# Sums of four softmax weights in all groups but the last batch's, and query and key stacks through a DRAM copy, in a planned graph-network kernel

## The chip, the cores and the metric

One core of one Trainium2 chip runs the whole program. Time is device microseconds of one execution. The engines named below: PE is the tensor engine (PEld are its weight loads), DVE the vector engine, ACT the scalar engine, POOL the GpSimd engine, SP the engine that issues most of the DMAs. SBUF and PSUM are the on-chip memories, DRAM the memory outside the core.

## What is computed

Sixteen graphs (batches) of 1024 nodes with 256 features, all with one 1024 x 1024 adjacency matrix, go through four layers, each on `relu(layernorm(x))` with a residual. Layers 0 to 2 are graph attention layers (4 heads, 1 head, 1 head). Layer 3 is the one that the change touches; cut to what matters:

```
x -> h = max(layernorm(x), 0)
q, k, v = split(h @ w_qkv), 8 heads of 32
scores  = q k^T / sqrt(32), where(adj > 0, scores, -1e9)
t       = softmax(scores) @ v
y       = layernorm(h + t);  f = relu(y @ w1 + b1) @ w2 + b2
x + layernorm(y + f)
```

All is in float32.

## The kernel before

`direct` builds the kernel. It doesn't issue instructions in the order of the source: it records pieces of work, each with its engine, an assumed duration, the buffers that it reads and writes, and a place in a stream. `Record.schedule` then goes through a model of the engines and writes the order in which all of them are issued, for every engine. Engines work through their own list in order. The constants `PASS`, `SLACK`, `BIAS`, `LEAD` and the lists in `KNOTS` (one per stream, interpolated along the stream) set priorities and assumed delays; the streams of one batch's graph layers (`gat0` to `gat2`) and of another batch's layer 3 (`values`, `steps`, `feed`) run beside each other. The last batch has no other beside it.

Layer 3 (`attention`) works in four groups per batch: two sets `g` of four heads, and two halves `hf` of the 512 queries each. A group has eight steps `jt`, one for each 128 keys. A step makes the scores of four heads (L1352, on PE), their exponentials (L1376, on ACT) into two tiles `pa` of 128 x 2 x 512, and the product with the 0/1 mask (L1385, on DVE). Two steps later the weights are used twice on PE, each time by a "quad": four narrow matmuls of 32 columns each that lie side by side (L1217, eight instructions, as a float32 matmul is two).

- One quad multiplies them with the values, for each step.
- Another multiplies them with `ones`, which gives the softmax's denominators. It need not see each step alone: `run_of` says how many steps' weights are added up first, in a pair of tiles `sums`. The first two are added on DVE (L1244), and each further one by an accumulating DMA that POOL issues (L1253), two DMAs per step, one for each tile of the pair. There is one pair of `sums`, with two tiles, which the next run takes over after the quad.

Before, a run has 4 steps in the groups with `hf` = 1 and 2 steps in those with `hf` = 0; in the last batch there is no adding.

The scores' operands are stacks: queries and keys are split into a rounded part `hi` and a rest `lo` and laid over each other on the partitions, four blocks `a` of 32 rows (queries hi, hi, lo, lo; keys hi, lo, hi, lo), for each of the four heads `r`. `project` makes one half of them: a matmul (L1132), `hi` on ACT (L1141), `lo` on DVE (L1144), and then 16 DMAs on SP's queue, one for each block and head, from SBUF to SBUF (L1154). There are 8 projections per batch. `hi` and `lo` have one buffer each, the keys' stack `ks` one and the queries' stack `qs` two.

Other work on the queues: SP also issues the stores of graph attention's rows to DRAM (L843, `rd<-rt`), their broadcast back to all partitions (L852, `row<-rd`, which L868 on DVE waits for), loads of `x`, and the feed-forward part's loads and stores (L1502, L1574). POOL also computes the layer norms' powers (L466, L481) and some sums of the range watch (L511, L820).

Of the kernel before, what the change touches and what calls it, by code (L numbers as in the profile page):

```python
# [113 lines left out]


WEIGHT = {"pe": 1.0, "dve": 0.3}
PASS = {"pe": 0.198, "act": 0.153, "dve": 0.202, "pool": 0.13, "dma": 0.0}


class Work:  # L120


    def __init__(self, engine, us, emit, key, modes, moved, lands):
        self.engine, self.us, self.emit, self.key, self.modes = engine, us, emit, key, modes
        self.pass_on = PASS[engine]
        self.moved = moved
# [9 lines left out]
def priority(x):  # L136
    base, knots, total, lead = x.stream
    at = x.pos / max(total, 1e-9) * (len(knots) - 1)
    k = max(0, min(int(at), len(knots) - 2))
    key = base + knots[k] + (knots[k + 1] - knots[k]) * (at - k)  # L140
    return round(key - (LEAD.get(x.engine, 0.0) if lead else 0.0), 6)


class Record:
# [44 lines left out]
    def schedule(self):  # L189
        for n, x in enumerate(self.work):  # L190
            x.n = n
            if x.key is None:
                x.key = priority(x)
            x.left = len(x.before)
            for y in x.before:
                y.after.append(x)
        free = dict.fromkeys(PASS, 0.0)
        queue = 0.0
        future = {e: [] for e in PASS}
        now = {e: [] for e in PASS}  # L200
        mode = "full"
        for x in self.work:
            if not x.left:
                heapq.heappush(future[x.engine], (x.ready, x.n, x))

        def opening(x):

            at, need = 0.0, {}
            for buf in x.opens:
                need[buf.ring] = need.get(buf.ring, 0) + 1  # L210
            for ring, n in need.items():
                if len(ring.free) < n:
                    return None
                at = max(at, sorted(ring.free)[n - 1][0])
            return at

        def turn(x):

            return BIAS * SWITCH.get((mode, x.modes[0]), 0.0) if x.engine == "pe" else 0.0

        def choose(e):

            at = free[e]
            while future[e] and future[e][0][0] <= at:
                x = heapq.heappop(future[e])[2]
                heapq.heappush(now[e], (x.key, x.n, x))
            best = None
            for key, n, x in now[e]:
                t = opening(x)
                if t is not None:  # L230
                    best = min(best or (1e9,), (max(at, t), key + turn(x), n, x))
            if future[e] and (best is None or future[e][0][0] < best[0]):
                for t, n, x in sorted(future[e]):
                    if opening(x) is not None:
                        t = max(t, at, opening(x))
                        best = min(best or (1e9,), (t, x.key + turn(x), n, x))
                        break
            return best

        order = []  # L240
        while True:
            choices = [(c, e) for c, e in ((choose(e), e) for e in PASS) if c]
            if not choices:
                break
            (at, _, n, x), e = min(choices, key=lambda c: c[0][0])
            if (x.key, n, x) in now[e]:
                now[e].remove((x.key, n, x))
                heapq.heapify(now[e])
            else:
                future[e].remove((x.ready, n, x))  # L250
                heapq.heapify(future[e])
            for buf in x.opens:
                _, k = heapq.heappop(buf.ring.free)
                buf.k, buf.t = k, buf.ring.tiles[k]
            us = x.us
            if e == "pe":
                us += SWITCH.get((mode, x.modes[0]), 0.0)
                mode = x.modes[1]
            x.start = at
            if x.moved:  # L260
                queue = max(at + (us if e == "pool" else 0.2), queue) + x.moved
                us = max(us, queue - at - AHEAD)
                x.pass_on = queue + x.lands + SLACK - (at + us)
            order.append(x)
            free[e] = at + us
            for buf in x.shared:
                buf.end = max(buf.end, at + us + x.pass_on)
                buf.uses.remove(x)
                if not buf.uses:
                    heapq.heappush(buf.ring.free, (buf.end, buf.k))  # L270
            for y in x.after:
                y.ready = max(y.ready, at + us + (x.pass_on if y.before[x] else 0.0))
                y.left -= 1
                if not y.left:
                    heapq.heappush(future[y.engine], (y.ready, y.n, y))
        assert len(order) == len(self.work)
        self.end = max(free.values())
        return order


AHEAD = 3.5
SLACK = 0.56
KNOTS = {
    "gat0": (-6.706, -3.534, -2.307, -1.522, -2.815),
    "gat1": (0.005, 0.503, 0.618, 0.731, 0.916),
    "gat2": (0.938, 0.468, 0.637, 0.867, 1.15),
    "beside": (0.241, 1.203, 1.943, 0.54, 4.121),
    "values": (1.06, -3.362, -0.305, 3.145, 0.767),
    "steps": (1.014, 1.448, 1.59, 2.064, 1.794),
    "feed": (2.016, 2.165, 2.509, 2.154, 2.609),  # L290
    "last": (2.808, 3.335, 3.547, 5.206, 6.138),
}
BIAS = 1.225
LEAD = {"act": 9.55, "dve": -0.732}

SWITCH = {
    ("full", "col4"): 0.137,
# [23 lines left out]
def mm_us(n):  # L321
    return 2 * max(2 * n / 2.4 + 3.0, 109) / 1000
# [5 lines left out]
def direct(ctx, tc, flag, x, adj, gat_w, gat_a, w_qkv, ln1_g, ln1_b, ln2_g, ln2_b, w1, b1, w2, b2, out):  # L328


    nc = tc.nc
    NB, N, C = x.shape
    NT = N // P
    CT = C // P
    HALF = N // 2
    TH = NT // 2
    D3 = C // H3
    HG = P // D3
# [31 lines left out]
    def ring(name, n, shape, pool=work):  # L370
        return Ring([pool.tile([P] + shape, F32, name=f"{name}{i}") for i in range(n)])
# [32 lines left out]
    dram = ctx.enter_context(tc.tile_pool(name="dram", bufs=1, space=DRAM))  # L404
    r_x3 = ring("x3", 3, [NT, C], dram)
    r_rd = ring("rd", 4, [P], dram)
    r_rt = ring("rt", 1, [P])
    r_sc = ring("sc", 4, [HALF], psum)
    r_bank = Shared([psum.tile([P, HALF], F32, name=f"bank{i}") for i in range(4)])
# [8 lines left out]
    def pe(us, emit, w, r, modes=("full", "full")):  # L418
        rec.add("pe", us, emit, w, r, modes)

    def act(us, emit, w, r):
        rec.add("act", us, emit, w, r)
# [7 lines left out]
    def dma(moved, lands, emit, w, r, key=None, us=0.57, engine="dma"):  # L430
        rec.add(engine, us, emit, w, r, key=key, moved=moved, lands=lands)
# [650 lines left out]
    def attention(b, xt, b_mv, b_rstd):  # L1082
# [42 lines left out]
        def project(g, hf, keys, stack, at):  # L1125

            sc, hi, lo = r_sc.new(), r_hi.new(), r_lo.new()
            c0 = keys * C + g * P

            def product():  # L1130
                for ct in range(CT):
                    nc.tensor.matmul(  # L1132
                        sc.t,
                        wqkv_sb[:, ct, c0 : c0 + P],
                        hT.t[:, ct, hf * HALF : (hf + 1) * HALF],
                        start=ct == 0,
                        stop=ct == CT - 1,
                    )

            pe(CT * mm_us(HALF), product, [sc], [b_qkv] + [hT((ct, hf)) for ct in range(CT)])  # L1140
            act(act_us(HALF), lambda: nc.scalar.copy(hi.t.bitcast(F32R), sc.t), [hi], [sc])  # L1141
            dve(
                tt_us(HALF),
                lambda: nc.vector.tensor_sub(lo.t, sc.t, hi.t),  # L1144
                [lo],
                [sc, hi],
            )
            for a in range(4):
                part = ((hi, hi, lo, lo), (hi, lo, hi, lo))[keys][a]
                for r in range(HG):  # L1150
                    dma(
                        0.3,
                        1.5,
                        lambda: nc.sync.dma_start(  # L1154
                            stack.t[a * D3 : (a + 1) * D3, r, at : at + HALF],
                            part.t[r * D3 : (r + 1) * D3, :],
                        ),
                        [stack((r, hf if keys else 0, a))],
                        [part],
                        us=0.59,  # L1160
                    )

        def values(it):
            sc = r_sc.new()
# [47 lines left out]
        steps = [(g, hf, jt) for g in range(CT) for hf in range(2) for jt in range(NT)]  # L1212
# [11 lines left out]

        def run_of(g, hf):

            return 1 if b == NB - 1 else 4 if hf == 1 else 2

        rec.stream(b, KNOTS["steps"])
        GROUP = 2  # L1230
# [1 line left out]
        for n in range(len(steps) + LAG):  # L1232
            m = n - LAG
            if m >= 0:
                g, hf, jt = steps[m]
# [12 lines left out]
                elif jt % run:  # L1248
                    for ss, pt in zip(sums[g, hf], pas[m]):
# [6 lines left out]
                            us=1.135,  # L1256
# [81 lines left out]
            if n < len(steps):  # L1338
                g, hf, jt = steps[n]
# [928 lines left out]
```

## Time and profile before

| What | Value |
|---|---|
| Median of 3 runs | 4092.49 us (4090.72 to 4097.2) |
| The profiled execution | 4091.28 us, its span 4089.5 us |
| Mean granted clock of PE | 0.995 |
| PE: sum quads of `sums` with `ones` | 1440 instructions, 193.4 us busy |
| DVE: adds into `sums` | 360, 430.3 us |
| POOL: accumulating DMAs | 240, 512 KB each |
| SP: copies for the stacks | 2048, 64 KB each |

How to read it: busy time of an engine is the time in which an instruction of it ran; a matmul's end is modelled and matmuls overlap, so the time that a matmul costs PE is read from start to start. In lines of the groups the parts are line, engine, operation, out<-in, shapes, count, then busy time in us and mean ns of one, then the idle time of the engine ahead of them and what ended it. In lines of the waits: who waited, for whom, the total in us, how often, the longest. In lines of a timeline: start in us, duration, engine, line, operation, out<-in, shape, count.

### The profile page before, as it was taken

Reading aid. Unit: us, or ns where it says so; the run is one execution under the profiler, and the core shown is the slowest. Engines: PE = TensorE matmul, PEld = TensorE weight load, DVE = VectorE, ACT = ScalarE, POOL = GpSimd, SP = SyncE. Lnnn points to the kernel's source line nnn. Section 1 sums busy time; section 2 is a strip of 40 time slices with the busy share of each in tenths; the row PEclk is TensorE's granted clock in tenths of the full one; section 3 lists DMA queues with packets and bytes.
Section 4 is the critical chain, followed back from the end, with each engine's and each line's share of the span. In section 5 each row is a group of like instructions: output and inputs, shape, how many; then the busy total and the mean of one; then the engine's idle time right before and its main releaser. Section 6 shows DMA issues by size and latency. Waiting matters only on the chain.

```text
span 4089.5 us, 68377 instructions
## 1 busy us (share of the span) xinstructions
PE 4023.3 (98%) x23874; PEld 2354.7 (58%) x23874; DVE 3499.0 (86%) x5994; ACT 2689.9 (66%) x6673; POOL 646.7 (16%) x631
## 2 busy tenths in 40 slices
PE   7999999999999999999999999999999999999998
PEld 3566466564655646566564665646556465665643
DVE  7768898988979799897988989889797998979866
ACT  5467676775757767576675767757577675765765
POOL 1102011121211202111121211212111011111100
PEclk9999999999999999999999999999999999999999
DMA  3024344343444324443243443434443244432441
GB/s 128 24 77 102 99 109 99 89 93 98 101 112 102 90 75 112 114 108 90 77 105 99 109 105 87 95 92 103 110 109 85 74 112 113 108 90 59 107 103 47
DMA packets 215248, 389.65 MB, mean 95 GB/s; under 512 B 45168, under 2 KB 80240, under 8 KB 214896
## 3 DMA queue, kind: packets, MB, share of 16 engines
q1 hardware_dynamic: 180336, 259.36, 22.4%
q0 software_dynamic: 34560, 125.84, 16.2%
q8 instruction: 191, 3.13, 0.3%
q14 instruction: 161, 1.32, 0.1%
HBM read 91.03 MB, written 33.95 MB: 31 GB/s over the span
## 4 chain that ended last, share of the span: by engine, by line
PE 85%; DVE 5%; ACT 4%; SPq 2%; DMA 2%; issue 1%; POOL 1%; DVEq 0%; ACTq 0%; POOLq 0%
PE bank L895 20%; PE bank L1217 14%; PE sc L1352 11%; PE bank L982 9%; PE bank L770 9%; PE bank L529 6%; PE bank L992 5%; PE bank L1449 4%; PE sc L1132 4%; PE sc L1169 2%; SPq L1154 2%; DVE pt L868 2%; DVE pa L1385 1%; POOL rstdz L466 1%; ACT waste L446 1%
## 5 line engine op out<-in xcount | busy, mean ns | idle before, releaser
L1385 DVE TENSOR_TENSOR pa<-pa,mask 128x1024 f32<-128x1024 f32 x1024 | 1221.4, 1218 | 72.4 <-ACT pa L1376 69.4
L1376 ACT ACTIVATE pa<-sc 128x512 f32<-128x512 f32 x2048 | 1098.3, 606 | 234.2 <-PE sc L1352 175.1
L868 DVE SCALAR_TENSOR_TENSOR pt<-row,e,mask 128x512 f32<-128x512 f32 x1472 | 1016.3, 744 | 62.2 <-DMA row<-rd 40.3
L895 PE MATMUL bank<-qb,pt 128*128 128x257 f32 x4096 | 942.0, 380 | 3.5 <-ACT fz L1533 3.5
L895 PEld LDWEIGHTS bank<-qb,pt 128*128 128x128 f32 x4096 | 771.3, 189 | 147.1 <-ACT pa L1376 12.6
L1352 PE MATMUL sc<-qs,ks 128*128 128x512 f32 x2048 | 717.7, 455 | 11.2 <-DMA qs<-lo 5.8
L1217 PE MATMUL bank<-pa,va 128*32 128x512 f32 x4096 | 504.8, 596 | 0.3 <-DVE pa L1385 0.2
L1352 PEld LDWEIGHTS sc<-qs,ks 128*128 128x128 f32 x2048 | 360.4, 189 | 212.3 <-ACT pa L1376 56.5
L1244 DVE TENSOR_TENSOR sums<-pa,pa 128x1024 f32<-128x1024 f32 x360 | 430.3, 1219 | 57.6 <-PE bank L1217 57.4
L982 PE MATMUL bank<-pt,qb 128*32 128x512 f32 x3840 | 468.7, 597 | 2.4 <-DVE pt L868 1.4
L770 PE MATMUL bank<-w_aug,hT 128*128 128x259 f32 (+1 forms) x1504 | 383.1, 393 | 0.5 <-ACT hT L764 0.5
L1253 POOL DMA_DIRECT2D sums<-pa x240 | 210.1, 878 | 930.5 <-DVE pa L1385 507.2
L770 PEld LDWEIGHTS bank<-w_aug,hT 128*128 128x128 f32 x1504 | 275.8, 191 | 121.1 <-ACT pa L1376 13.7
L923 ACT ACTIVATE ex<-bank,rec 128x256 f32<-128x256 f32 x256 | 122.1, 477 | 294.5 <-DVE rec L915 287.6
L982 PEld LDWEIGHTS bank<-pt,qb 128*32 128x32 f32 x3840 | 118.8, 109 | 275.9 <-issue 193.0
L1217 PEld LDWEIGHTS bank<-pa,va 128*32 128x32 f32 x4096 | 120.5, 109 | 263.0 <-issue 227.6
L992 PE MATMUL bank<-pt,e 128*32 128x512 f32 x1920 | 258.5, 592 | 0.0
L500 ACT ACTIVATE hn<-xh,mv,rstd 128x256 f32<-128x256 f32 x376 | 195.9, 592 | 93.0 <-DVE mv L490 89.1
L1132 PE MATMUL sc<-hTa,wqkv_sb 128*128 128x512 f32 x512 | 244.4, 600 | 0.1
L466 POOL TENSOR_TENSOR rstd<-rstd,neg_half 128x4 f32<-128x4 f32 x96 | 138.5, 1443 | 597.0 <-DVE rstd L458 588.3
L820 POOL TENSOR_TENSOR sum_e<-sum_e,e 128x12 f32<-128x12 f32 (+1 forms) x94 | 114.7, 1220 | 648.2 <-ACT e L781 648.1
L1141 ACT CAST hi<-sc 128x512 fp32r<-128x512 f32 x128 | 74.8, 585 | 196.4 <-PE sc L1132 72.8
(152 smaller groups left out, 4638.4 us busy)
## 6 DMA issues: line engine op xcount, KB each, us to landing
sums<-pa POOLq DMA_DIRECT2D x240, 512.0 KB, 6.0
row<-rd SPq DMA_DIRECT2D x184, 256.0 KB
ks<-hi SPq DMA_DIRECT2D x512, 64.0 KB
ks<-lo SPq DMA_DIRECT2D x512, 64.0 KB
qs<-hi SPq DMA_DIRECT2D x512, 64.0 KB
qs<-lo SPq DMA_DIRECT2D x512, 64.0 KB
xh<-in_x_dram SPq DMA_DIRECT2D x32, 512.0 KB
x<-xh SPq DMA_DIRECT2D x32, 512.0 KB
```

The lines of the kernel that those rows point to most:

```text
L529: nc.tensor.transpose(dst(k), src(k), ident[:shape, :shape])
L770: nc.tensor.matmul(g.t[:, : C + 3 * H], hT.t[:, ct, k * P : (k + 1) * P], w_aug[l][:, ct, :], start=ct == 0, stop=ct == CT - 1,)
L868: lambda: nc.vector.scalar_tensor_tensor(pt.t, row.t, e3[:, 2, jt // TH, h, jt % TH : jt % TH + 1], mask[:, jt, hf * HALF : (hf + 1) * HAL ...
L895: nc.tensor.matmul(g.t[:, : D + 1], pts[jt].t[:, k * P : (k + 1) * P], qb[:, jt, 0, :], start=jt == 0, stop=jt == NT - 1,)
L982: nc.tensor.matmul(g.t[u * D + d : u * D + d + D3, :], qb[:, j, h + u, d : d + D3], pts[u][j - jt].t, start=j == 0, stop=j == NT - 1,)
L992: nc.tensor.matmul(gd.t[c : c + D3, :], one(jt + k, h + u).to_broadcast([P, D3]), pts[u][k].t, start=jt == 0, stop=jt == NT - 2,)
L1132: nc.tensor.matmul(sc.t, wqkv_sb[:, ct, c0 : c0 + P], hT.t[:, ct, hf * HALF : (hf + 1) * HALF], start=ct == 0, stop=ct == CT - 1,)
L1217: nc.tensor.matmul(ac.t[r * D3 : (r + 1) * D3, :], columns(r), of_head(r), start=first, stop=last,)
L1244: lambda: nc.vector.tensor_add(ss.t, p0.t, p1.t),
L1352: nc.tensor.matmul(scs[r - r0].t, ks.t[:, r, jt * P : (jt + 1) * P].bitcast(F32R), q.t[:, r, :].bitcast(F32R), start=True, stop=True,)
L1376: lambda: nc.scalar.activation(pt.t[:, v, :], sc.t, AF.Exp, scale=1.0 / math.sqrt(D3)),
L1385: lambda: nc.vector.tensor_mul(pt.t, pt.t, mask[:, jt : jt + 1, i0 : i0 + HALF].to_broadcast([P, 2, HALF]),),
```

## The change

Runs are 4 steps in all groups of all batches but the last, which still adds nothing. `project` stores `hi` and `lo` to a DRAM buffer `hl` (two DMAs) and loads each of the four blocks `a` for all four heads at once from there (four DMAs); SP still issues them all. The planner's constants are others, most of its lists of knots have nine entries in place of five, and its rule for DMAs differs: where a DMA of SP would find the modelled queue more than `BEHIND` us behind, it is assumed to hold SP for `HELD` us, in place of the earlier rule with `AHEAD`.

```diff
-PASS = {"pe": 0.198, "act": 0.153, "dve": 0.202, "pool": 0.13, "dma": 0.0}
+PASS = {"pe": 0.168, "act": 0.548, "dve": 0.19, "pool": 0.13, "dma": 0.0}
...
             if x.moved:
+                if e == "dma" and queue - at > BEHIND:
+                    us = max(us, HELD)
                 queue = max(at + (us if e == "pool" else 0.2), queue) + x.moved
-                us = max(us, queue - at - AHEAD)
                 x.pass_on = queue + x.lands + SLACK - (at + us)
...
-AHEAD = 3.5
-SLACK = 0.56
+BEHIND, HELD = 2.0, 1.35
+SLACK = 0.748
 KNOTS = {
...
-    "steps": (1.014, 1.448, 1.59, 2.064, 1.794),
+    "steps": (0.801, 1.295, 1.336, 1.535, 1.758, 1.892, 2.342, 1.964, 2.258),
...
-BIAS = 1.225
-LEAD = {"act": 9.55, "dve": -0.732}
+BIAS = 1.1
+LEAD = {"act": 10.244, "dve": 1.51}
...
+    r_hl = ring("hl", 3, [2, HALF], dram)
...
+            hl = r_hl.new()
+            for k, part in enumerate((hi, lo)):
+                dma(0.65, 1.5, lambda: nc.sync.dma_start(hl.t[:, k, :], part.t), [hl(k)], [part])
             for a in range(4):
-                part = ((hi, hi, lo, lo), (hi, lo, hi, lo))[keys][a]
-                for r in range(HG):
-                    dma(
-                        0.3,
-                        1.5,
-                        lambda: nc.sync.dma_start(
-                            stack.t[a * D3 : (a + 1) * D3, r, at : at + HALF],
-                            part.t[r * D3 : (r + 1) * D3, :],
-                        ),
-                        [stack((r, hf if keys else 0, a))],
-                        [part],
-                        us=0.59,
-                    )
+                k = ((0, 0, 1, 1), (0, 1, 0, 1))[keys][a]
+                dma(
+                    1.0,
+                    1.83,
+                    lambda: nc.sync.dma_start(
+                        stack.t[a * D3 : (a + 1) * D3, :, at : at + HALF],
+                        hl.t[:, k, :].rearrange("(r d) n -> d r n", r=HG),
+                    ),
+                    [stack((r, hf if keys else 0, a)) for r in range(HG)],
+                    [hl(k)],
+                )
...
         def run_of(g, hf):
 
-            return 1 if b == NB - 1 else 4 if hf == 1 else 2
+            return 1 if b == NB - 1 else 4
```

## The prediction

> **What bounds the kernel now.** I read the page's busy times first, then five equal stretches in the middle, then the tensor engine's (PE's) timeline, then the DMA views, then the waits.
>
> ```profile
> PE 4023.3 (98%) x23874; PEld 2354.7 (58%) x23874; DVE 3499.0 (86%) x5994; ACT 2689.9 (66%) x6673; POOL 646.7 (16%) x631
> ```
>
> Of the span of 4089.5 us PE is without work for 66.2 us. The stretches say where: one batch takes about 248 us, and a stretch of that length from the middle shows
>
> ```profile
> 1618.00:1866.00 248.00, 247.44 (x1483) 146.65 (x1483) 219.31 (x374) 167.92 (x419) 41.13 (x41) 1.00 0.41 99
> ```
>
> PE 247.44 of 248.00 us, at a granted clock of 1.00, VectorE (DVE) 219.31, ScalarE 167.92, the DMA engines 0.41 of the time. So in the middle there is 0.6 us per batch to win from better feeding; the idle 66 us lie mostly in the first 100 us and the last 200. Anything that leaves PE's list of work shortens the batch, as long as nothing else comes to feed it late.
>
> Matmuls overlap, so "busy" might hide gaps. The timeline's starts settle that:
>
> ```profile
> 1507.27 1.04 PE L770 MATMUL bank<-w_aug,hT 128*128 128x259 f32 x4
> 1507.95 0.82 PE L1352 MATMUL sc<-qs,ks 128*128 128x512 f32 x2
> 1508.70 1.06 PE L1217 MATMUL bank<-sums,ones 128*32 128x512 f32 x8
> 1509.70 2.02 PE L770 MATMUL bank<-w_aug,hT 128*128 128x259 f32 x8
> 1511.36 0.82 PE L1352 MATMUL sc<-qs,ks 128*128 128x512 f32 x2
> 1512.02 1.08 PE L770 MATMUL bank<-w_aug,hT 128*128 128x259 f32 x4
> ...
> 1520.17 1.92 PE L1217 MATMUL bank<-pa,va 128*32 128x512 f32 x16
> 1521.91 1.12 PE L1217 MATMUL bank<-sums,ones 128*32 128x512 f32 x8
> 1522.77 1.12 PE L1217 MATMUL bank<-pa,va 128*32 128x512 f32 x8
> ```
>
> The reader is to take one price from this: what a quad of sums (eight instructions, `sums` against `ones`) holds PE for. Between two other quads it is 1522.77 - 1521.91 = 0.86 us. Alone among wide matmuls it is 1509.70 - 1508.70 = 1.00 us, and the two scores ahead of it take 1508.70 - 1507.95 = 0.75 us where the same two ahead of L770 take 1512.02 - 1511.36 = 0.66 us: alone, 1.09 us. Over the whole timeline I count 181 stretches of such quads, 60 of them alone on both sides. Starts follow starts by the work's own steps nearly everywhere; steps over 0.75 us too long are rare between 300 and 3700 us.
>
> Now a rule that speaks against this reading. The Trainium skill (Perfetto Trace Analysis, Identifying the Most-Contended Engine) holds that matmul busy time is a poor measure of room on TensorE and that the busy share of weight loads is a better one; here that share is 58%, and by it some 40% of the span would be open and the change would win nothing by taking quads away. I go by the starts above, which leave no such room.
>
> **The change, part by part.** *Sums of four steps.* `run_of` now gives 4 instead of 2 for the groups with hf = 0, in 15 batches, 2 per batch: 30 groups of 8 steps. Each then has 2 sum quads instead of 4: 60 quads leave PE. With a third of them alone (60 of 181) that is 20 x 1.09 + 40 x 0.86 = 56.2 us; bounds are 51.6 (none alone) and 65.4 (all alone). All of it lies on the path that sets the end.
>
> The adds fall from 8 to 4 per group, 120 fewer:
>
> ```profile
> L1244 DVE TENSOR_TENSOR sums<-pa,pa 128x1024 f32<-128x1024 f32 x360 | 430.3, 1219 | 57.6 <-PE bank L1217 57.4
> L1253 POOL DMA_DIRECT2D sums<-pa x240 | 210.1, 878 | 930.5 <-DVE pa L1385 507.2
> ```
>
> 120 x 1.219 = 146 us less on DVE. I cost this at nothing: DVE is at 88% in the middle and PE does not wait for it there. If PE's cover went, DVE would now be the further from the limit.
>
> In their place come 8 accumulating DMAs per group, 240 more. On POOL's queue 240 x 0.878 = 211 us, from 16% to 21% of the span. Behind them in POOL's queue stand the small powers of the layer norms (L466, L481) that a graph layer's start waits for; a DMA whose `pa` is not masked yet, or whose predecessor into the same `sums` has not landed, holds them. Today POOL waits 16.5 us in all for a predecessor, in 5 places; twice that is 33 us over 15 batches, all on an engine that idles 80%. I take nothing, with an upper bound of 33 us.
>
> ```profile
> q1 hardware_dynamic: 180336, 259.36, 22.4%
> q0 software_dynamic: 34560, 125.84, 16.2%
> ...
> sums<-pa POOLq DMA_DIRECT2D x240, 512.0 KB, 6.0
> ```
>
> Queue q0 is these DMAs alone; doubling it adds another 16.2% of the 16 DMA engines.
>
> The quads wait for the landings, which the view of tile `sums` gives:
>
> ```profile
> DMA to landing us min/median/max: 4.4/6.0/8.9
> ```
>
> From the timelines of POOL and PE I took, for each of the 60 four-step runs, the time from the issue of its last DMA to its quad: 6.1 us to 12.0 us, middle 9.2, 24 of them under 8.9. PE's weight loads lost 1.3 us in all to these landings. So four-step runs already work in half of the groups at next to no cost on PE, and the others have the same form, with the same two buffers of `sums` per run. I take no wait.
>
> By the page DMA: Bandwidth & Descriptors of the Trainium skill (Anatomy of one DMA) such a transfer takes about 2.0 us plus its bytes at 436 GB/s, here some 3.2 us. By that figure no quad could ever come too early; the trace's 6.0 and 8.9 us decide, since here 24 runs have less than the longest landing in hand.
>
> *Stacks through DRAM.* A projection's stack now takes 2 stores of 256 KB to DRAM and 4 loads of 256 KB instead of 16 copies of 64 KB; 128 projections. SP issues 768 instead of 2048. The old ones take 0.589 us each, 9.4 us per projection; the new ones at 0.37 (row loads) to 0.59 take 2.2 to 3.5 us. The second half's chain was 8 x 0.589 us of issue and a landing; it becomes a store, its landing, two loads and theirs. SP now waits for the store. The nearest rows:
>
> ```profile
> SPq L1502 <- DMA out_dram<-xr: 85.2, 48, 3.7
> SPq L852 <- DMA rd<-rt: 41.1, 49, 1.1
> PE sc L1352 <- DMA qs<-lo: 5.8, 1, 5.8
> DVE pt L868 <- DMA row<-rd: 40.3, 42, 2.0
> ```
>
> The first is SP behind a store of the same 256 KB to DRAM: 85.2 / 48 = 1.78 us, at most 3.7; I take it as the nearer one (the second is 8 KB or 2 KB: 0.84 us). What queues behind SP then is above all the row loads (L852) that the graph layers' weights wait for, 40.3 us of DVE's time now, all behind PE's full list. In the middle the chain gets shorter by 5.9 to 7.2 us of issue and longer by about 1.8 us plus a load's landing: no cost. Where nothing else is left for PE, in the last batch, the stack shows: PE stood 5.8 us there for `qs`. Bounds: that goes (-6 us), or each of the last batch's 8 projections costs 1.78 us more (+14 us). I take +2. `hi` and `lo`, one buffer each, come free after one store instead of 8 copies. The DMA engines: 64 MB more through q1, by q1's own 259.36 MB in 22.4%, is 5.8%. Together 0.39 + 0.16 + 0.06 = 0.61 of the time on average (0.39 from the two rows), in the fullest slices, now 0.49, about 0.75.
>
> *New plan.* The order is new everywhere. What it can win in the middle is 0.6 us per batch and the changes between narrow quads and wide matmuls: 397 entries into quads in the timeline, at (1.00 - 0.86) + (0.75 - 0.66) = 0.23 us, 91 us; 10% either way is 9 us. I take zero.
>
> *Sum.* The profiled execution took 4091.3 us, 1.8 over its span and 1.2 under the median of the runs. 4091.3 - 56.2 + 2 = 4037.1; on the median's footing one more: 4038. Bounds of this case: 4091.3 - 65.4 - 6 - 9 = 4011, and 4091.3 - 51.6 + 14 + 9 = 4063.
>
> **Rivals.** *Late landings (slower).* The sum quads wait on PE for accumulating DMAs, since q0's load has doubled. PE works in order, so the whole batch stands. If every last DMA landed at the 8.9 us that is the longest now, today's 60 runs would wait 38.4 us in all (8.9 less each of the 24 shorter times); 120 runs 77 us: 4035 + 77 = 4112. It decides from a mean wait of 56 / 120 = 0.47 us per run. For: q0 at 32% and the engines at 0.61. Against: 1.3 us of such waits now, and in the slice with the engines at 0.49 PE is busy 101.74 of 102 us.
>
> *Part given back.* DVE waits for rows behind heavier DMA traffic, POOL's powers held: half of POOL's 33 us bound and half of the 40.3 us of row waits again, 37 us, reach PE: 4038 + 37 = 4075. Against: DVE got 146 us of air.
>
> *The plan gives it back.* The sums leave, but the new order leaves PE as much idle as it saves, or more entries: 4092. For: the plan carries new constants throughout. Against: a list with 56 us less and the same dependences should have a shorter order.
>
> **How the numbers follow.** Forecast 0.60, part given back 0.12, no net change 0.04, late landings 0.24. A measurement of this kernel can tell about 0.2% (8 us) from no change. Faster by more: 0.60 + 0.12 = 0.72; within: 0.04; slower: 0.24. The likeliest case alone runs from 4011 to 4063; to leave out no more than 2 in 10 the range goes on through the middle cases to just past the late landings' 4112: 4011 to 4116.
>
> **What would show it.** Right: 120 instead of 180 sum quads in those groups (960 instead of 1440 instructions), 240 adds, 480 accumulating DMAs, batches of about 244.5 us (248 less 4 quads of 0.86 to 1.09), PE at 98% with busy time down by some 55 us, q0 at about 32%. Wrong: PE or its weight loads waiting on L1253 or on the `sums` landing by tens of us, landings over 9 us, stretches with PE well under the full 247 of 248; or more entries into quads at the same busy share. A stall of more than 10 us in the first or last 200 us would put the stacks' term wrong.

## The result, and the profile after

The change made the kernel slower by 0.4%: the median is 4108.88 us (4101.97 to 4112.2, 7 runs) against 4092.49 us, the ratio 1.0038 with a 95% interval of 1.0027 to 1.0050. The profiled execution has a span of 4108.4 us, at a mean granted clock of 0.996 (before 0.995).

First the busy times, the DMA engines' slices and the two queues, from the page:

```profile
PE 4000.8 (97%) x23394; PEld 2338.2 (57%) x23394; DVE 3363.7 (82%) x5874; ACT 2683.3 (65%) x6673; POOL 812.7 (20%) x871
...
DMA  3066675665766656666566766657566575665661
...
q0 software_dynamic: 69120, 251.69, 32.1%
q1 hardware_dynamic: 192624, 326.39, 28.1%
```

What was removed is gone: 480 instructions of PE, 120 of DVE with 135 us, and q0 has doubled. But PE's idle time is 4108.4 - 4000.8 = 107.6 us, where it was 66.2. The groups (the first from the groups by form, the others from the page) show the edit itself as expected, and 12.6 us in which PE stood ahead of a sum quad. Before, by the same view:

```profile
L1217 PE MATMUL bank<-sums,ones 128*32 128x512 f32 x1440 | 193.4, 601 | 0.1
```

After:

```profile
L1220 PE MATMUL bank<-sums,ones 128*32 128x512 f32 x960 | 143.2, 598 | 12.6 <-DMA sums<-pa 12.6
...
L1247 DVE TENSOR_TENSOR sums<-pa,pa 128x1024 f32<-128x1024 f32 x240 | 288.3, 1218 | 40.7 <-PE bank L1220 40.1
L1256 POOL DMA_DIRECT2D sums<-pa x480 | 422.4, 883 | 1957.6 <-PE sc L1355 442.8
```

The stretch of one batch that the prediction showed, 1618 to 1866 us, now reads (columns: stretch, its length, busy of PE, PEld, DVE, ACT, POOL, granted clock, share of the DMA engines, GB/s):

```profile
1618.00:1866.00 248.00, 243.76 (x1432) 142.49 (x1434) 207.76 (x363) 164.09 (x412) 51.00 (x56) 1.00 0.64 148
```

PE is without work for 4.2 us of it, where it was 0.6. What PE waits for, from its own waits:

```profile
PE bank L984 <- DVE pt L870: 17.0, 14, 7.0
PE bank L531 <- DVE pa L628: 15.1, 2, 10.8
PE bank L897 <- ACT ex L925: 13.1, 13, 1.1
PE bank L1220 <- DMA sums<-pa: 12.6, 13, 1.5
PE sc L1134 <- ACT pa L1379: 7.1, 8, 2.0
```

The second is the start. The third and fourth have 13 occurrences each, about one per batch: new waits that recur at the same places. Short waits hide behind the modelled ends of matmuls, so I also took every start-to-start time on PE's timeline and subtracted what the work itself takes, by the same prices for both kernels: beyond work and changes of shape PE loses, by this estimate, 71 us before and 139 us after. Work is shorter by 52 us (60 quads of 0.86), stalls longer by 68. In the middle that is close to nothing per batch before and about 6 us after.

One such place, on POOL's timeline and then on PE's:

```profile
1595.10 0.92 POOL L1256 DMA_DIRECT2D sums<-pa  x1 [6.54 <-DVE reca L1315]
1596.33 0.86 POOL L1256 DMA_DIRECT2D sums<-pa  x1 [0.32 <-issue]
1605.56 0.86 POOL L1256 DMA_DIRECT2D sums<-pa  x1 [8.37 <-issue]
1608.05 0.88 POOL L1256 DMA_DIRECT2D sums<-pa  x1 [0.52 <-ACT qb L794]
...
1610.34 1.03 PE L1220 MATMUL bank<-sums,ones 128*32 128x512 f32 x4
1612.77 1.05 PE L1220 MATMUL bank<-sums,ones 128*32 128x512 f32 x4 [1.41 <-DMA sums<-pa]
```

The first two are step three of a run, the next two step four into the same tiles. POOL can issue step four only when step three has landed. The first DMA of step three landed 9.9 us after its issue (the view of `sums` for that moment), and step four follows half a microsecond later, at 1605.56: over 10 us after step three. The first half of the quad runs, the second half waits for the last landing: PE loses 2 us. What the DMA engines did in that time, in stretches of 10 us:

```profile
1575.00:1585.00 10.00, 9.24 (x37) 6.30 (x36) 9.87 (x15) 8.01 (x24) 2.30 (x4) 1.00 1.04 220
1585.00:1595.00 10.00, 10.00 (x68) 6.30 (x68) 8.59 (x19) 8.65 (x21) 1.85 (x2) 1.00 0.85 239
1595.00:1605.00 10.00, 10.00 (x53) 7.68 (x52) 8.32 (x15) 5.27 (x12) 1.78 (x2) 1.00 1.00 215
1605.00:1615.00 10.00, 8.59 (x47) 4.66 (x51) 4.97 (x6) 7.80 (x26) 4.07 (x5) 1.00 0.60 115
```

They are full or nearly so (1.04, 0.85, 1.00) for 30 us, and PE stalls at their end. The page's slice of 100 us shows 6 tenths there. Cut into 660 stretches of 5 us from 400 to 3700 us, the engines are at 0.9 or more in 13% of them before, in 33% after.

### The profile page after: what moved, and what is told of

It is laid out like the page before. It is cut to its first block, busy times and chain, and to the rows that moved or that the text cites. A ratio compares the mean times of both kernels' runs of the same rounds, so it can differ in the third digit from the quotient of the medians.

```text
span 4108.4 us, 65744 instructions
## 1 busy us (share of the span) xinstructions
PE 4000.8 (97%) x23394; PEld 2338.2 (57%) x23394; DVE 3363.7 (82%) x5874; ACT 2683.3 (65%) x6673; POOL 812.7 (20%) x871
## 3 DMA queue, kind: packets, MB, share of 16 engines
q1 hardware_dynamic: 192624, 326.39, 28.1%
## 4 chain that ended last, share of the span: by engine, by line
PE 65%; DVE 16%; DMA 10%; ACT 5%; issue 3%; POOL 1%; SPq 0%; DVEq 0%; ACTq 0%; POOLq 0%
PE bank L897 15%; PE bank L1220 10%; PE sc L1355 8%; PE bank L984 7%; PE bank L772 6%; DVE pt L870 6%; PE bank L531 5%; DVE pa L1388 4%; PE sc L1134 4%; PE bank L994 3%; DMA sums<-pa 3%; PE bank L1452 3%; DMA out_dram<-xr 3%; PE sc L1172 2%; ACT pa L1379 2%
## 5 line engine op out<-in xcount | busy, mean ns | idle before, releaser
L1379 ACT ACTIVATE pa<-sc 128x512 f32<-128x512 f32 x2048 | 1111.3, 603 | 349.9 <-PE sc L1355 157.9
L870 DVE SCALAR_TENSOR_TENSOR pt<-row,e,mask 128x512 f32<-128x512 f32 x1472 | 1012.4, 747 | 75.3 <-DMA row<-rd 41.3
L897 PE MATMUL bank<-qb,pt 128*128 128x257 f32 x4096 | 949.7, 382 | 13.8 <-ACT ex L925 13.1
L897 PEld LDWEIGHTS bank<-qb,pt 128*128 128x128 f32 x4096 | 765.2, 189 | 191.5 <-issue 28.8
L1256 POOL DMA_DIRECT2D sums<-pa x480 | 422.4, 883 | 1957.6 <-PE sc L1355 442.8
L1355 PE MATMUL sc<-qs,ks 128*128 128x512 f32 x2048 | 703.5, 451 | 2.7 <-issue 1.9
L1220 PE MATMUL bank<-pa,va 128*32 128x512 f32 x4096 | 527.0, 598 | 1.2 <-DVE pa L1388 1.2
L984 PE MATMUL bank<-pt,qb 128*32 128x512 f32 x3840 | 476.9, 597 | 17.5 <-DVE pt L870 17.0
L772 PE MATMUL bank<-w_aug,hT 128*128 128x259 f32 (+1 forms) x1504 | 381.1, 392 | 12.9 <-DVE xh L954 6.5
L772 PEld LDWEIGHTS bank<-w_aug,hT 128*128 128x128 f32 x1504 | 274.2, 190 | 146.7 <-issue 34.3
L1247 DVE TENSOR_TENSOR sums<-pa,pa 128x1024 f32<-128x1024 f32 x240 | 288.3, 1218 | 40.7 <-PE bank L1220 40.1
L984 PEld LDWEIGHTS bank<-pt,qb 128*32 128x32 f32 x3840 | 122.3, 109 | 290.8 <-issue 182.2
L1220 PEld LDWEIGHTS bank<-pa,va 128*32 128x32 f32 x4096 | 111.8, 109 | 242.6 <-issue 212.4
L448 ACT ACTIVATE waste<-xh,mv 128x256 f32<-128x256 f32 x384 | 196.3, 511 | 6.8
L502 ACT ACTIVATE xh<-xh,mv,rstd 128x256 f32<-128x256 f32 x256 | 137.8, 604 | 27.5 <-DVE mv L492 26.2
```

The costliest lines, as they stand in the source:

```text
L502: lambda: nc.scalar.activation(dst, src, func, bias=bias, scale=scale),
L772: nc.tensor.matmul(g.t[:, : C + 3 * H], hT.t[:, ct, k * P : (k + 1) * P], w_aug[l][:, ct, :], start=ct == 0, stop=ct == CT - 1,)
L870: lambda: nc.vector.scalar_tensor_tensor(pt.t, row.t, e3[:, 2, jt // TH, h, jt % TH : jt % TH + 1], mask[:, jt, hf * HALF : (hf + 1) * HAL ...
L897: nc.tensor.matmul(g.t[:, : D + 1], pts[jt].t[:, k * P : (k + 1) * P], qb[:, jt, 0, :], start=jt == 0, stop=jt == NT - 1,)
L984: nc.tensor.matmul(g.t[u * D + d : u * D + d + D3, :], qb[:, j, h + u, d : d + D3], pts[u][j - jt].t, start=j == 0, stop=j == NT - 1,)
L1220: nc.tensor.matmul(ac.t[r * D3 : (r + 1) * D3, :], columns(r), of_head(r), start=first, stop=last,)
```

## The experiments

Two theories at the start: *load* (the heavier DMA traffic lands late and makes PE's feeders late) and *order* (the new order is bad by itself). Most runs keep the changed kernel's order of instructions and change only what one kind of DMA moves. They were taken in five groups, each with the kernel before beside it (medians 4092.94 to 4096.18 us), to which the ratios refer; so times of different groups compare to some 4 us only.

**Narrow accumulating DMAs.**

```diff
-lambda: nc.gpsimd.dma_start(ss.t, pt.t, accum_op=ALU.add),
+lambda: nc.gpsimd.dma_start(ss.t[:, 0, :P], pt.t[:, 0, :P], accum_op=ALU.add),
```

> The changed kernel with every instruction in the same order, but each of the 480 accumulating DMAs moves 128 of its 1024 columns (so a part of the denominators is left out). Theory load: the doubled traffic of these DMAs lands late and makes the sum quads, the rows and through them DVE and ACT late, so nearly all of the about 6 us of new PE stall per batch goes: 4109 - 15 x 5 to 6 = 4020 to 4035 us. Theory order: the new order itself places DVE and ACT work too late for PE; only the waits for the landings themselves go (12.6 us at PE, 27.5 us at its weight loads): 4080 to 4097 us.

Measured 4032.49 us, ratio to before 0.9847 (0.9831 to 0.9864). Load, fully: the same order is 76 us faster.

**No accumulating DMAs** (`lambda: None` in their place).

> The same order again, with the 480 accumulating DMAs left out altogether (steps three and four of each run are missing from the denominators), so POOL also issues nothing for them and its powers and range sums have nothing ahead of them. If holding POOL's queue is a part of the loss, this is faster than the run with narrow DMAs by 5 us or more; if only transport matters, within 5 us of it.

Measured 4029.92 us (0.9843, 0.9826 to 0.9859), 2.6 us from the run before: holding POOL's queue cost next to nothing (the two intervals overlap).

**Narrow stacks.**

```diff
+            wide = HALF if b == 0 else P
...
-nc.sync.dma_start(hl.t[:, k, :], part.t)
+nc.sync.dma_start(hl.t[:, k, :wide], part.t[:, :wide])
...
-stack.t[a * D3 : (a + 1) * D3, :, at : at + HALF], hl.t[:, k, :]
+stack.t[a * D3 : (a + 1) * D3, :, at : at + wide], hl.t[:, k, :wide]
```

> The changed kernel in the same order, with the stores and loads of the stacks cut to 128 of 512 columns in all batches but the first (the other columns keep old values). Theory load: the stacks' 28.1% share of the DMA engines falls by about 10 points, rows and accumulating DMAs land earlier: 4080 to 4100 us. Theory order: 4105 to 4112 us.

Measured 4023.91 us (0.9827, 0.9811 to 0.9844): the gain, 85 us, is far larger than I expected and larger than that of the narrow accumulations, with those at full width (q0 32.8%, q1 15.3%). Either of the two transfers, made narrow, ends the loss. Each of these cuts goes below what the kernel before moved: q0 to 6.5% in the first run (16.2% before the change), q1 to 15.3% here (22.4%). The waits cross over: DVE's wait for the reload of `x` (on SP's queue q1), first of the kernel before, then of the changed kernel, with narrow accumulations (q0) and with narrow stacks (q1):

```profile
DVE xr L1508 <- DMA xr<-x: 12.0, 4, 4.4
```

```profile
DVE xr L1511 <- DMA xr<-x: 75.8, 32, 5.2
```

```profile
DVE xr L1511 <- DMA xr<-x: 26.9, 25, 3.9
```

```profile
DVE xr L1512 <- DMA xr<-x: 16.4, 19, 3.7
```

The Trainium skill (DMA: Bandwidth & Descriptors, Issuing engines are not separate DMA queues) says that DMAs of all issuing engines interleave on the same 16 engines; these rows agree: narrowing q0's DMAs took this wait for a load of q1 from 75.8 to 26.9 us.

**More load on the kernel before.** Its order, and 240 further accumulating DMAs that nobody reads:

```diff
+def add():
     nc.vector.tensor_add(ss.t, p0.t, p1.t)
+    if run == 2:
+        nc.gpsimd.dma_start(extra[u], wqkv_sb[:, :, :HALF], accum_op=...)
```

> The kernel before in its own order, with 240 further accumulating DMAs of 512 KB, one beside each DVE add of the two-step groups, from the constant weights into a DRAM scratch that nobody reads. Theory load: about 16% more of the DMA engines delays rows, stacks and landings, so the old order loses 20 to 60 us: 4110 to 4150 us. Theory order: the old order has enough slack, 4090 to 4098 us.

Measured 4217.67 us (1.0305, 1.0288 to 1.0322): 121 us slower, beyond both ranges. The granted clock was 0.988 here, so some 0.7% or 29 us of that may be the clock. PE's stalls rose, by the same estimate, from 71 to 191 us. The old order is no more tolerant of load than the new one, as far as DMAs into DRAM, at places that nothing foresaw, can be compared with the change's own.

**Half-width accumulating DMAs** (`ss.t[:, 0, :]`, `pt.t[:, 0, :]`).

> The changed kernel in the same order, each of the 480 accumulating DMAs moves half of its columns (the other half is left out of the denominators). Theory load: the loss depends steeply on the DMA engines' share; with q0 at about 18 to 20 instead of 32 points the stalls are mostly gone: 4035 to 4060 us. If the loss were proportional to the bytes: about 4075 us. If the number of these DMAs and not their bytes counted: 4100 to 4110 us.

Measured 4034.02 us (0.9851, 0.9835 to 0.9868), with all 480 DMAs and q0 at 17.7%, near the 16.2% before the change: as good as none. The loss isn't proportional to bytes: the first half of them costs some 4 us, which the intervals don't tell from none, the second 75. Stretches of 5 us at 0.9 or more: 14%.

**POOL adds by itself**, in all steps three and four, then in step three alone:

```diff
-lambda: nc.gpsimd.dma_start(ss.t, pt.t, accum_op=ALU.add),
+lambda: nc.gpsimd.tensor_tensor(out=ss.t, in0=ss.t, in1=pt.t, op=ALU.add),
```

> The changed kernel in the same order, but all 480 accumulating DMAs are elementwise adds that POOL itself computes from the same tiles (the output is complete). Theory load (the DMA engines' share of 0.61 makes rows, loads and landings late): q0 is empty, so the time goes to that of the narrow DMAs, 4025 to 4045 us, if an add of 128 x 1024 on POOL takes under some 3 us and does not slow DVE. Rival, POOL: the adds take much longer than the 0.88 us of issuing or hold DVE off, and PE waits for sums as before or more: over 4100 us.

> The same order; in each run the third step is added by POOL itself and only the fourth by an accumulating DMA (output complete, 240 DMAs as before the change). Theory load: half of q0's rise goes, 8 of 32 + 28 points twice over 16, and most of the loss with it: 4030 to 4060 us. Rival, POOL: as above, over 4090 us.

Measured 4889.53 us (1.194, 1.192 to 1.196) and 4483.99 us (1.0954, 1.0936 to 1.0972): the rival. The groups of the first:

```profile
L1256 POOL TENSOR_TENSOR sums<-sums,pa 128x1024 f32<-128x1024 f32 x480 | 1380.4, 2887 | 1541.1 <-DVE pa L1388 845.4 <-DVE sums L1247 314.0 <-DVE rec L1044 171.9
...
L1388 DVE TENSOR_TENSOR pa<-pa,mask 128x1024 f32<-128x1024 f32 x1024 | 1470.3, 1458 | 57.9 <-ACT pa L1379 48.3 <-ACT mvz L444 8.2
```

An add takes 2.9 us, and DVE's masks beside it 1.458 us on average in place of 1.219. DVE now holds the pace (50% of the chain that ended last, where it was 16%), so in this order it is no way to save the DMAs. The granted clock was lower too, 0.951 and 0.979 in the two runs, so a part of the loss may be the clock.

**DVE adds step three**, in the groups with `hf` = 0, then in all four-step groups, at the places where POOL would have issued:

```diff
-lambda: nc.gpsimd.dma_start(ss.t, pt.t, accum_op=ALU.add),
+lambda: nc.vector.tensor_add(ss.t, ss.t, pt.t) if jt % run == 2 and hf == 0 else nc.gpsimd.dma_start(...),
```

> The changed kernel with all other work in the same order; in the groups with hf = 0 the third step of a run is added by DVE in place of the accumulating DMA, at the place where POOL would have issued it (120 adds of 1.22 us, 120 DMAs fewer, output complete). Theory load: q0 falls from 32 to about 24 points, the DMA engines from 0.61 to about 0.52, where the half-width DMAs (0.47) showed no loss: 4040 to 4070 us, faster than before. Rival, DVE: 146 us of DVE work that the order did not foresee makes masks and weights late: 4090 to 4130 us.

> As the run before, but the third step is added by DVE in all four-step groups (240 adds, 293 us of DVE; 240 DMAs, as many as before the change; output complete). Theory load alone would give 4030 to 4050 us; DVE goes from 82 to about 90% of the span, so I expect DVE to be late in the slices that are already at 0.95: 4060 to 4110 us. If it is faster than the run with hf = 0 alone, the DMA traffic is the worse of the two costs.

Measured 4161.42 us (1.0170, 1.0153 to 1.0187) and 4263.54 us (1.0416, 1.0399 to 1.0434): the rival, by a wide margin. Both expectations were misses, far under the times. DVE at 84% has room on average; that it has none where an add comes unplanned is what the waits suggest (PE's wait for `pt` from DVE, L984, went from 17.0 to 35.8 us in the first run).

**The same with an order planned for it** (other `KNOTS`, `BIAS` and `LEAD`, the third add recorded as DVE's work):

> The changed kernel with the third step added by DVE in the groups with hf = 0 (as in the run with 120 such adds), but with an order planned for it: other knots, bias and leads. Same DMA bytes as that run (q0 about 24 points). Theory load plus order: without the surprise for DVE the same work and traffic go well under before, 4045 to 4080 us; if 0.52 of the DMA engines is already too much, or the plan leaves DVE at its limit, 4090 to 4130 us.

Measured 4090.82 us (0.9989, 0.9979 to 0.9999), 71 us under the unplanned one, and no faster than before in any useful sense. Its DMA engines are at 0.9 or more in 28% of the 5 us stretches, between 13% before and 33% after the change; the time is that of the kernel before and 18 us under the changed one. It is inconclusive on how much of this is order and how much traffic.

**Stacks from SBUF to SBUF again**, in the changed order:

```diff
-lambda: nc.sync.dma_start(hl.t[:, k, :], part.t)
+lambda: None
...
-nc.sync.dma_start(stack.t[a * D3 : (a + 1) * D3, :, at : at + HALF], hl.t[:, k, :]...)
+for r in range(HG):
+    nc.sync.dma_start(stack.t[a * D3 : (a + 1) * D3, r, at : at + HALF], part.t[r * D3 : (r + 1) * D3, :])
```

> The changed kernel in the same order, with the stacks copied from SBUF to SBUF as before the change: nothing is stored to DRAM, and in the place of each of the four loads stand four copies of 64 KB. Theory load: q1 falls from 28 to about 22.5 points, the DMA engines from 0.61 to about 0.55: part of the loss goes, 4050 to 4095 us. Rival, SP: sixteen issues of 0.59 us that the order did not foresee block rows behind them: over 4105 us.

Measured 4427.52 us (1.0814, 1.0796 to 1.0832): the rival, some 320 us above its bound, at a granted clock of 0.967. DVE's wait for rows rose from 41.3 to 205.2 us; sixteen issues stand where the order foresaw four, and `hi` and `lo` stay taken longer than it assumed (some copies probably find the next projection's values). It says that this order can't do without the DRAM buffer, and nothing on the buffer's price.

**Three blocks.** The product lo times lo is left out, its block zero and never loaded:

```diff
-lambda: nc.sync.dma_start(
+lambda: a < 3 and nc.sync.dma_start(
```

> The changed kernel in the same order, with the stacks' fourth block (lo times lo, the smallest of the four products) set to zero once and never loaded: three loads per projection instead of four, 32 MB or about 2.8 points less on q1. Theory load, with a loss that sets in steeply between 0.47 and 0.61 of the DMA engines: at about 0.575 a quarter to a half of the 75 us comes back, 4070 to 4090 us. If the loss hung on the transfers' number or on the stores' landing alone: 4100 to 4110 us.

Measured 4041.90 us (0.9873, 0.9856 to 0.9889): it beats both kernels, by 52 and 67 us, and gains more than either range said. q1's share went only from 28.1 to 25.3%, and stretches of 5 us at 0.9 or more went from 33 to 27%, so the count of full stretches doesn't price the loss by itself. The same place of a batch, POOL's timeline (28.6 us earlier in the span) and the 10 us stretches (27 us earlier):

```profile
1566.52 0.92 POOL L1258 DMA_DIRECT2D sums<-pa  x1 [6.75 <-DVE reca L1317]
1567.76 0.86 POOL L1258 DMA_DIRECT2D sums<-pa  x1 [0.32 <-issue]
1574.92 0.86 POOL L1258 DMA_DIRECT2D sums<-pa  x1 [6.30 <-DVE rec L919]
1577.41 0.87 POOL L1258 DMA_DIRECT2D sums<-pa  x1 [1.40 <-ACT pa L1381]
```

```profile
1548.00:1558.00 10.00, 10.00 (x43) 7.59 (x42) 9.69 (x16) 9.45 (x29) 2.75 (x3) 1.00 1.03 227
1558.00:1568.00 10.00, 10.00 (x69) 6.34 (x67) 8.56 (x20) 8.42 (x18) 2.02 (x3) 1.00 0.81 227
1568.00:1578.00 10.00, 10.00 (x52) 7.67 (x51) 7.14 (x14) 5.46 (x15) 2.30 (x4) 1.00 0.88 175
1578.00:1588.00 10.00, 10.00 (x63) 5.05 (x63) 6.82 (x8) 9.83 (x30) 2.07 (x4) 1.00 0.47 94
```

Step four follows step three by 8.40 us in place of 10.46, and PE is busy for 10.00 of 10.00 in the stretch where it lost 1.4 us (from start to start its sum quad still takes some 0.3 us too long). A quarter of the loads is enough to bring this burst to an end in time.

Is it the traffic? Three more runs. **The kernel before with three blocks:**

> Control for the run with three blocks: the kernel before, its order unchanged, with the stacks' fourth block zero and not copied (12 copies per projection in place of 16). PE has no stall to lose here, so leaving the block out should do nothing by itself: 4085 to 4094 us. If it gains 30 us or more, the gain of three blocks is not relief of the changed kernel's traffic.

Measured 4068.80 us (0.9938, 0.9922 to 0.9955). A miss in part: 25 us come even there, so the kernel before was not free of such a cost either, though its page showed PE full. Whether the bytes did it or the 512 issues that SP no longer makes isn't separated; DVE's wait for rows fell from 40.3 to 21.0 us. Between the two kernels with three blocks the change is worth 4068.8 - 4041.9 = 27 us.

**One more DMA per projection**, from `hl` to a DRAM scratch, after the fourth load:

```diff
+if a == 3:
+    nc.sync.dma_start(more[keys], hl.t[:, k, :])
```

> The opposite dose: the changed kernel in the same order with one further DMA of 256 KB per projection, from the DRAM buffer to a DRAM scratch that nobody reads, so about as much more traffic as the three-block run had less. Theory bursts (the stretches in which the DMA engines are full grow long, and what is queued in them lands late): the loss goes on steeply, 4150 to 4220 us. If the step from three to four blocks was some other effect of the fourth load: 4105 to 4125 us.

Measured 4144.84 us (1.0125, 1.0108 to 1.0141): 36 us more than the changed kernel, a little under the first range: less steep than I expected upwards. So the loss isn't tied to the fourth block. This DMA and the fourth load each take a place in SP's list as well; narrow stacks, with every issue kept, are the run that shows the bytes.

**Quads that don't read the sums:**

```diff
-lambda r: ss[r // 2].t[:, r % 2, :],
+lambda r: ones[:, :1].to_broadcast([P, HALF]),
```

> The changed kernel with the same order and the same DMAs, but the sum quads multiply a constant in place of sums (the denominators are wrong), so PE waits for no landing and a run's sums wait for no quad. If the loss comes to PE through the sums' landings and what they hold: 4030 to 4050 us. If it comes through late rows, loads and the adds that hold their pa: 4075 to 4100 us.

Measured 4085.36 us (0.9978, 0.9968 to 0.9989; 4076.94 to 4096.63 in 10 runs), in the second range. With all DMAs in place and no wait for a landing on PE, 24 us come back: about a third of the 75. (DVE's adds no longer wait for the quads either, 40.1 us in the changed kernel, so the 24 us are the price of both.) The rest reaches PE by other ways. In this run's waits of PE the place of the sums is gone and the others stand:

```profile
PE bank L984 <- DVE pt L870: 14.8, 14, 7.0
PE bank L772 <- DVE xh L954: 14.7, 7, 3.2
PE bank L897 <- ACT ex L925: 14.5, 14, 1.1
```

These are DVE's and ACT's work for the graph layers. The first is no part of the loss: the run with narrow accumulations has it too (14.4 us, 14 times). The other two are: that run has 1.3 us of the second and none of the third. In the changed kernel's trace they can be followed back. One place, on the timelines of SP, DVE, ACT and PE:

```profile
1059.31 0.40 SPq L1577 DMA_DIRECT2D out_dram<-xr  x1
1064.97 0.34 SPq L1505 DMA_DIRECT2D xr<-x  x1
...
1067.61 0.69 DVE L1511 TENSOR_TENSOR xr<-xr,row_c 128x512 f32<-128x512 f32 x1 [3.80 <-DMA xr<-x]
1075.09 0.16 DVE L917 RECIPROCAL rec<-bank 128x1 f32<-128x1 f32 x1
...
1075.35 0.47 ACT L925 ACTIVATE ex<-bank,rec 128x256 f32<-128x256 f32 x1 [1.93 <-DVE rec L917]
...
1075.87 2.01 PE L897 MATMUL bank<-qb,pt 128*128 128x257 f32 x8 [1.14 <-ACT ex L925]
```

SP can't issue the reload of `x` until a store of results has landed, here 5.6 us after its issue. DVE stands 3.80 us for the reload and is then busy without a gap up to `rec`, which ACT and then PE wait for. All 17 waits of these two kinds in the changed kernel (13 of L897 for `ex`, 4 of L772 for `xh`) have such a stand of DVE, of 2.3 us or more, 7 to 10 us ahead of them. SP's own waits for these stores:

```profile
SPq L1505 <- DMA out_dram<-xr: 191.3, 62, 6.2
```

They were 85.2 us before the change, and are 142.4 us with narrow and 148.6 us with half-width accumulations and 121.0 us with narrow stacks. DVE's wait for rows, in contrast, hardly grew: 40.3 us before, 41.3 us after. No run takes the reload's wait away alone, so how much of the 50 us goes this way is not measured.

## Why the prediction was wrong

*PE's list: right.* 60 quads left, 52 us of work, and wherever the traffic was cut the time showed a gain: 4024 to 4042 us in five runs, around the 4035 that the sum had without waits. That they come so near is partly luck. Those runs also cut traffic that the kernel before had, and with three blocks in both kernels the change gives 27 us; what a kernel before without any such cost would take no run shows. The new order also enters quads 426 times in place of 397, 29 x 0.23 = 7 us by the prediction's own price, within its bound of 9. So the reading of PE as full was right in the main. The weight loads' share was 58% before and 57% after; by it, the rule of the Trainium skill (Perfetto Trace Analysis, Identifying the Most-Contended Engine) would have promised nothing from these quads, and these runs speak against that reading.

*"I take no wait": the step that failed.* Two errors in it. First, I looked from the last DMA of a run to its quad, 6.1 to 12.0 us. That step four's DMA itself waits for step three's landing I saw, but priced it on POOL's queue alone, at nothing, and not on the quad's path; the pair is what grows, 8.40 us with three blocks and 10.46 in the burst above. Nor were the 5 places in which POOL was seen to wait the measure of it: by the landings in the traces, 74 of the 120 DMAs of fourth steps before the change, and 177 of 240 after, were issued within 0.65 us of the landing that they needed. Second, I took landings from a trace with engines at 0.41 for one at 0.61. The longest landing went from 8.9 to 12.9 us while the median fell to 5.4:

```profile
DMA to landing us min/median/max: 4.4/5.4/12.9
```

The page DMA: Bandwidth & Descriptors of the Trainium skill (Anatomy of one DMA) gives 2.0 us plus bytes at 436 GB/s. The narrow DMAs of 64 KB had a median of 2.3 us, near the 2.15 that I estimate by it; at 512 KB a median of 5.4 us and 4.4 us at best stand against an estimate of 3.2.

*The traffic: summed right, read wrong.* 0.61 and "about 0.75 in the fullest slices" are what the profile after shows (60.2% on q0 and q1, slices of 5 to 7 tenths). But slices of 100 us are too coarse; in a third of the 5 us stretches the engines are at 0.9 or more. Of the terms that I costed at nothing POOL's issues were rightly so (2.6 us between narrow DMAs and none), and so, in total, were the waits for rows. What I left out is the reload of `x`: DVE's wait for it went from 12.0 to 75.8 us. The row that would have led there, SP behind the store of `out_dram<-xr`, I used only as the price of a stack's store.

*The rivals.* "Late landings" named the mechanism and 4112 us, 3 us from the result, but not for its reason: it put all 77 us on the sum quads, and these carry about 24. "Part given back" had a way through DVE, at 37 us, but by late rows and POOL's powers, where the trace shows the reload of `x`. Both kinds of wait happened together, about 75 us in all. The chance of 0.24 for slower was too small: two unknown waits on one shared resource are not alternatives. "The plan gives it back" falls: the same order runs in 4024 us.

*The stacks.* I costed them at +2, by their latency. PE waited for no stack after the change, and its idle time in the last 200 us fell from 26.0 to 18.7 us; what cost was their bytes, 5.7 points more on q1. Narrow stacks alone, 12.8 points less, gave 85 us back. (The 5.9 to 7.2 us by which I had the chain get shorter are SP's time for a whole projection; the chain that I named had 8 x 0.589 = 4.7 us of issue. Nothing hangs on it here.)

## What to carry to other kernels

When an edit trades the bound engine's work for DMA traffic, the average share of the DMA engines says little: cut the trace into stretches of some 5 us and look for where they are already full, because what is queued there lands late and an order written ahead can't move. Such a count shows where to look, not what it costs: at 27% the kernel with three blocks was 67 us faster than at 33%, and another order at 28% no faster than before. Take away either of two added transfers with the order held, at half width too, before blaming the order, and give the kernel before the same relief: leaving out a quarter of the stack loads decided between 0.4% slower and 1.3% faster than before, and leaving out the same block gave the kernel before 25 us as well. Of two DMAs that depend on each other, count both landings; and follow a wait of the bound engine back through the lists of the others, here from PE over ACT and DVE to a store that SP waited for.

## What was new on the hardware

An accumulating DMA of 512 KB landed in 4.4 us at best, with a median of 5.4 to 6.0, and in 12.9 us at worst. An elementwise add of 128 x 1024 in float32 took POOL 2.89 us; beside 480 of them DVE's masks of the same size went from 1.219 to 1.458 us on average and its SCALAR_TENSOR_TENSOR operations of 128 x 512 from 0.747 to 0.919, while its adds into `sums`, also 128 x 1024, only went from 1.218 to 1.276.
